# First attention's last output product moved into the second attention's first step, and two sets of flips given to TensorE

## The chip, the cores and the metric

One core of one Trainium2 chip runs the kernel. A core has five engines that work side by side and wait for each other through semaphores: TensorE (PE, matmuls and transposes, with a separate row PEld for its weight loads), VectorE (DVE), ScalarE (ACT), GpSimd (POOL) and SyncE (SP, which here only issues transfers). Transfers are issued by SP or POOL and run on the core's 16 DMA engines. The metric is device microseconds of one execution; the time of a kernel is the median of its runs.

## The reference, cut to what matters

```python
def reference(x, ...):                      # x: 8 batches x 128 tokens x 512
    x = x + attn(cond(x, cond_weight, adapter_ids), wq, wk, wv, wo)
    x = x + ffn(cond2(x, Wq, Wk, Wv, Wo, ..., k_cache, v_cache, block_table, cache_seqlens), ...)
    return x

# cond:  h = x[b] @ weight[adapter_ids[b]].T                   a gathered 512x512 matrix for each batch
# attn:  32 query heads and 8 key heads of 16, causal softmax, output product with wo (512x512)
# cond2: q, k, v from x; RMS norm and rotation of q and k; keys and values are 512 cached rows,
#        gathered by pages, and the 128 own ones; cached rows from cache_seqlens on are masked;
#        softmax over 640; 32 query heads and 8 key heads of 128; output product with Wo (4096 -> 512)
# ffn:   y @ kernel + bias + two low-rank terms, one of them chosen by a gate for each batch
```

All of it is float32.

## The kernel before, in words

The order of the instructions on every engine is the order in which the program text issues them; tiles come from pools with a fixed number of buffers, and a tile waits until the last readers of its buffer are done. Each queue, SP's and POOL's too, works in order.

**Set-up.** SP loads the adapter numbers and the first x, then the first attention's weights wk, wv and wq (`wq_sb`, 1 MB, L368), the norm weights and the FFN bias (L370 to L372). POOL gathers the four 256 KB parts of batch 0's conditioning matrix (L296, tiles `cw`), then those of batch 1, then loads `wo_sb` (1 MB, L355) and two further x.

**First attention**, two half steps for each batch b (`for k in range(2 * B + 1)`): conditioning product (L515, `hp`), query, key and value products (L531, L546, L553), scores with a causal mask (L584, L596), softmax on DVE and ACT (L605, L619, L628), the division on POOL (L630), transposes of the probabilities on PE (L639), the value product (L658) and, one batch later, `out_proj1` (L674 to L679): four products of the attention's result `oT1` with `wo_sb`, the sum with x on DVE, and a store of the sum, `x1`, to DRAM (`x1_kept`). `flip_x1` (L683) makes the transposed copy `x1T` that the second attention reads. The tiles of this half lie in the pools `p1w` and `p1`, which are closed before the second half opens `p2c` and `p2` over the same memory. The last batch's `out_proj1` and `flip_x1` stand just ahead of that, after `keys(0)` and around `own_keys(0)`. On the way the weights of the second attention's first two heads are loaded (`load_qkv`, `load_wo`), and the FFN's low-rank terms are merged (`merge_a`, `merge_b`, `merge_w`).

**Second attention**, one step for each of 64 units u, a unit being one key head of one batch; heads 2n and 2n+1 of a batch make a pair, whose cached keys and values come in one gather (L158, POOL). In step u stand, on PE's order: the scores of unit u (L871 against the cached keys, L878 against the own ones), with the query product of unit u+1 (L175) between them; its key and value product (L215); the value product of unit u-1 (L927); transposes of unit u+1's queries (L252) and own keys (L271); the output product of unit u-1 (L946), summed into `y_acc`. DVE masks and negates the scores (L884), ACT takes the exponentials and divides (L894, L862), and DVE and POOL rotate and scale unit u+1's queries and keys (L198 to L245).

Two kinds of 128x128 flips are made without PE. The probabilities: DVE transposes 32x32 blocks (L865, tile `flips`), and SP moves the blocks to their places with 16 transfers of 80 KB for each unit (L915, tile `pT`). The cached keys of a pair: DVE block transposes (L822, `turn_keys`), then 16 transfers of 32 KB on SP (L835, `move_keys`), in a step of its own for pair 1 (all sixteen in step 1) and eight for each step after. Only units 0 and 1 have their keys flipped by PE (`keys`, L263, copied by ACT, L265).

**The end.** When the last head of a batch is done, `ffn_flip` transposes `y_acc` (L959, L961), `ffn_lora` takes the low-rank product (L978), `ffn` the main one (L993, L994) and adds the residual, which `ffn_loads` has fetched back from DRAM (L967 to L971). For batch 7 these follow each other in three steps without any scores.

## Time and profile before

| | us |
|---|---|
| median of 3 runs | 1432.43 |
| lowest and highest | 1428.14, 1433.11 |
| the profiled execution | 1425.07 |
| its span | 1423.3 |
| PE busy in it | 1390.3 (98%) |
| DVE busy | 935.1 (66%) |
| ACT busy | 653.3 (46%) |
| POOL busy | 566.7 (40%) |
| from one step's value product to the next, typical | 17.8 |

The span runs from the first instruction of the program to the last; 1.8 us of the profiled execution lie around it. The typical step is read from the chain that ended last, where the value products (L927) of steps 6 and 7 start at 340.18 and 357.97. A line of the profile such as `L927 PE MATMUL op<-pT,vg` names the line of the kernel, the engine, the operation, and the tile written and those read, with buffer numbers left out. Idle time in brackets is that of the engine before the instruction, with what ended it; where a wait has several conditions, the profile names the one whose semaphore it saw last. PE's granted clock is a share of full speed.

### The profile page before, as it was taken

What the parts mean: (1) busy time and instruction counts of PE and PEld (TensorE: products, weight loads), DVE (VectorE), ACT (ScalarE), POOL (GpSimd) and SP (SyncE); (2) the same over time, 40 slices, a digit from 0 to 9 for tenths busy, and PEclk for the clock granted to TensorE, in tenths of its full rate; (3) what the DMA queues carried; (4) which work ended last, traced back from release to release, by engine and by line L of the source; (5) the groups of instructions that cost most, each with busy time, mean ns of one, the idle gap of its engine ahead of it and who ended that gap; (6) DMA issues with size and microseconds to landing.
All of it is one profiled execution on the core that took longest, in us unless ns stands there. A gap on an engine that the chain in (4) does not pass through costs nothing.

```text
span 1423.3 us, 20224 instructions
## 1 busy us (share of the span) xinstructions
PE 1390.3 (98%) x6192; PEld 895.2 (63%) x6192; DVE 935.1 (66%) x2270; ACT 653.3 (46%) x1514; POOL 566.7 (40%) x552
## 2 busy tenths in 40 slices
PE   6999998999999999999999999999999999999997
PEld 6877754566666666666666666666666666566654
DVE  4777856566666666666666666666666766566651
ACT  3655534444444444444444444444444444334440
POOL 5774342433333333333333333333333433333220
PEclk9999999999999999999999999999999999999999
DMA  6255112444444565444445654444456544444332
GB/s 205 76 157 195 43 47 65 140 118 119 118 118 118 163 189 153 119 119 118 119 119 159 195 150 119 119 118 118 121 163 192 158 109 125 136 116 115 104 109 66
DMA packets 159387, 181.84 MB, mean 128 GB/s; under 512 B 94960, under 2 KB 100336, under 8 KB 159280
## 3 DMA queue, kind: packets, MB, share of 16 engines
q1 hardware_dynamic: 144000, 137.02, 34.2%
q0 software_dynamic: 15280, 43.53, 10.8%
q8 instruction: 50, 0.82, 0.3%
q14 instruction: 57, 0.47, 0.1%
HBM read 75.57 MB, written 4.72 MB: 56 GB/s over the span
## 4 chain that ended last, share of the span: by engine, by line
PE 91%; SPq 3%; DVE 2%; issue 2%; DMA 1%; POOL 1%; ACT 1%; DVEq 0%; POOLq 0%; ACTq 0%
PE op L927 19%; PE qp L175 15%; PE sc L871 15%; PE yp L946 15%; PE kvp L215 7%; PE sc L878 4%; PE hp L515 2%; SPq L915 2%; PE qTp L252 2%; PE att L674 2%; PE fp L993 2%; PE pT1p L639 2%; PE qp L531 2%; PE o L658 1%; PE sc L596 1%
## 5 line engine op out<-in xcount | busy, mean ns | idle before, releaser
L884 DVE CUSTOM_DVE_ANT_0 pr<-sc,mask,nq 128x640 f32<-128x640 f32 x256 | 225.8, 883 | 141.0 <-PE sc L878 128.1
L894 ACT ACTIVATE pr<-pr,nm 128x640 f32<-128x640 f32 x256 | 211.8, 827 | 188.0 <-DVE nm L884 185.2
L871 PE MATMUL sc<-kT,qT 128*128 128x512 f32 x512 | 263.2, 596 | 1.9 <-ACT kTo L273 1.5
L175 PE MATMUL qp<-wq,x1T 128*128 128x512 f32 x512 | 251.2, 593 | 0.0
L927 PE MATMUL op<-pT,vg 128*128 128x256 f32 x1024 | 244.6, 382 | 5.6 <-DMA pT<-fl 5.6
L946 PE MATMUL yp<-wo,oT 128*128 128x512 f32 x512 | 231.0, 594 | 0.0
L201 POOL TENSOR_TENSOR qa<-qa,qb 128x512 f32<-128x512 f32 x64 | 81.8, 1278 | 370.0 <-DVE sums L861 370.0
L927 PEld LDWEIGHTS op<-pT,vg 128*128 128x128 f32 x1024 | 195.6, 192 | 33.6 <-issue 5.4
L862 ACT ACTIVATE pr<-pr,sums 128x640 f32<-128x640 f32 x256 | 208.4, 814 | 0.0
L865 DVE STREAM_TRANSPOSE fl<-pr 128x640 f32<-128x640 f32 x256 | 192.2, 807 | 1.2 <-DMA kT<-flk 1.0
L878 PEld LDWEIGHTS sc<-kTo,qT 128*128 128x128 f32 x512 | 96.8, 190 | 124.8 <-issue 103.9
L946 PEld LDWEIGHTS yp<-wo,oT 128*128 128x128 f32 x512 | 92.3, 190 | 93.3 <-issue 92.0
L158 POOL DMA_INDIRECT kg<-in_k_cache_dram,idx_kv x128 | 131.6, 1028 | 37.5 <-issue 36.8
L158 POOL DMA_INDIRECT vg<-in_v_cache_dram,idx_kv x128 | 128.4, 1003 | 35.6 <-issue 32.9
L871 PEld LDWEIGHTS sc<-kT,qT 128*128 128x128 f32 x512 | 88.1, 192 | 81.9 <-issue 76.3
L254 ACT COPY qT<-qTp 128x512 f32<-128x512 f32 x64 | 37.5, 586 | 206.7 <-PE qTp L252 206.7
L215 PEld LDWEIGHTS kvp<-wkv,x1T 128*128 128x128 f32 x512 | 97.3, 190 | 40.5 <-issue 30.1
L215 PE MATMUL kvp<-wkv,x1T 128*128 128x256 f32 x512 | 121.0, 379 | 0.0
L242 POOL TENSOR_TENSOR rs<-ss,minus_half 128x5 f32<-128x5 f32 x64 | 76.5, 1195 | 82.4 <-DVE ss L240 82.4
L175 PEld LDWEIGHTS qp<-wq,x1T 128*128 128x128 f32 x512 | 82.8, 191 | 31.5 <-issue 31.5
L878 PE MATMUL sc<-kTo,qT 128*128 128x128 f32 x512 | 99.3, 276 | 0.0
L273 ACT COPY kTo<-kTp 128x128 f32<-128x128 f32 x64 | 17.1, 267 | 167.3 <-PE kTp L271 167.3
(140 smaller groups left out, 1682.0 us busy)
## 6 DMA issues: line engine op xcount, KB each, us to landing
pT<-fl SPq DMA_DIRECT2D x1024, 80.0 KB
kT<-flk SPq DMA_DIRECT2D x496, 32.0 KB
wq<-in_wq_dram SPq DMA_DIRECT2D x8, 1024.0 KB
wo<-in_wo_dram SPq DMA_DIRECT2D x8, 1024.0 KB
wkv<-in_wkv_dram SPq DMA_DIRECT2D x8, 512.0 KB
x_kept<-x SPq DMA_DIRECT2D x8, 256.0 KB
kg<-in_k_cache_dram,idx_kv POOLq DMA_INDIRECT x128, 3.5
vg<-in_v_cache_dram,idx_kv POOLq DMA_INDIRECT x128, 3.6
```

What stands on the lines that cost most here:

```text
L158: nc.gpsimd.indirect_dma_start(out=dst[:, c].rearrange("p n d -> p (n d)"), out_offset=None, in_=src, in_offset=bass.IndirectOffsetOnAxis( ...
L175: nc.tensor.matmul(s["qp"][:].rearrange("p h d -> p (h d)"), x1T[b][:, c, :], weights[g][0][:, c, :], start=(c == 0), stop=(c == KC - 1),)
L201: nc.gpsimd.tensor_tensor(qa[:], qa[:], qb[:], ALU.add)
L215: nc.tensor.matmul(s["kp"][:], x1T[b][:, c, :], weights[g][1][:, c, :], start=(c == 0), stop=(c == KC - 1))
L862: nc.scalar.activation(prs[r][:], prs[r][:], AF.Copy, scale=sums[:, r : r + 1])
L865: nc.vector.transpose(s["flips"][:, :, :, r, :].rearrange("p b c j -> p c b j"), prs[r][:])
L871: nc.tensor.matmul(sc[:, : NBLK * P].rearrange("p (k j) -> p k j", j=32), s["qT"][:, r, :], s["kT"], start=True, stop=True,)
L878: nc.tensor.matmul(sc[:, NBLK * P : NK], s["qT"][:, r, :], s["kTo"][:], start=True, stop=True)
L884: nc.vector.tensor_tensor_reduce(out=pr[:], in0=sc[:, :NK], in1=mask[:], scale=s["nq"][:, r : r + 1], scalar=3.0e38, op0=ALU.add, op1=ALU.min,
L894: nc.scalar.activation(pr[:], pr[:], AF.Exp, bias=nm[:, r : r + 1], scale=-1.0, accum_out=sums[:, r : r + 1],)
L927: nc.tensor.matmul(ops[h][:, : 2 * S], cached(u, "vg", c) if c < NBLK else s["vo"][:], s["pT"][:, :, c, 2 * h : 2 * h + 2, :].rearrange("p ...
L946: nc.tensor.matmul(yp[:], s["oT"][:, r, :], weights[g][2][:, r, :], start=(r == 0), stop=(r == REP - 1))
```

## The change

Four things are edited.

1. *Set-up.* `wq_sb` is loaded by POOL, between the gathers of batch 0 and batch 1, and no longer by SP. The bias is loaded by SP in the first attention's step of batch 4, ahead of `merge_loads`.
2. *The last batch of the first attention.* Its result goes to a tile of its own, `oT_kept`. Its output product is no longer made before the second half, but in step 0, after the products of unit 1 (`out_proj_last`), and its transposed copy later in that step (`flip_last`). x is loaded for it again (`x_last`). `wo_sb` moves to the pool of the second attention's output weights, which has two buffers; so `load_wo(1)`, which stood in the first attention, comes at the end of step 0.
3. *The keys of pair 1* (units 2 and 3) are flipped by PE in step 1, like those of units 0 and 1; DVE's transposes and SP's sixteen transfers for them are gone.
4. *The end.* Unit 63's probabilities are flipped by PE (`flips_last`: five transposes a head, copied to `pT` by DVE and ACT in turn), two heads before the LoRA and output products of unit 62 and two after. `y_acc` of batch 7 is transposed without unit 63's part; unit 63's output product is taken the other way round (`out_proj_turned`, 16 products of 128x128), so that it can be added to the transposed tile. Two steps fewer are run.

```diff
+    oT_kept = one([P, REP, S], F32, "oT_kept")
...
     def keys(u):
         s = st[u]
-        if u > 1:
-            return
...
-        wo_sb = p1w.tile([P, REP, DM], F32, tag="wo_sb", name="wo_sb")
+        wo_sb = wpool.tile([P, REP, DM], F32, tag="wo", name="wo_sb")
...
         gather_w(0)
+        nc.gpsimd.dma_start(out=wq_sb[:], in_=wq1.rearrange("(c p) e -> p c e", p=P))
         gather_w(1)
         nc.gpsimd.dma_start(out=wo_sb[:], in_=wo1.rearrange("(r p) e -> p r e", p=P))
...
-        nc.sync.dma_start(out=wq_sb[:], in_=wq1.rearrange("(c p) e -> p c e", p=P))
...
-        nc.sync.dma_start(out=bias[:], in_=ffn_b.unsqueeze(0).to_broadcast([P, DM]))
...
-                oT[b] = p1.tile([P, REP, S], F32, tag="oT1", name=f"oT1_{b}")
+                oT[b] = p1.tile([P, REP, S], F32, tag="oT1", name=f"oT1_{b}") if b + 1 < B else oT_kept
...
                 elif b == 3:
                     load_qkv(1)
-                    load_wo(1)
...
                 if b == 4:
+                    nc.sync.dma_start(out=bias[:], in_=ffn_b.unsqueeze(0).to_broadcast([P, DM]))
                     merge_loads()
         keys(0)
-        out_proj1(B - 1)
         own_keys(0)
         for i in range(2, KC):
             merge_w(i)
-        flip_x1(B - 1)
...
+    x_last = p2c.tile([P, DM], F32, tag="res", name="x_last")
+    nc.sync.dma_start(out=x_last[:], in_=x[B - 1])
+
+    def out_proj_last():
+        ps = p_mm.tile([P, DM], F32, tag="mm", name="att1_last")
+        for r in range(REP):
+            nc.tensor.matmul(
+                ps[:], oT_kept[:, r, :], wo_sb[:, r, :], start=(r == 0), stop=(r == REP - 1)
+            )
+        x1 = tile_a([P, DM], "x1_last")
+        nc.vector.tensor_tensor(x1[:], ps[:], x_last[:], ALU.add)
+        nc.sync.dma_start(out=x1_kept[B - 1][:], in_=x1[:])
+        return x1
+
+    def flip_last(x1):
+        tp = p_tp.tile([P, KC, S], F32, tag="tp", name="x1Tp_last")
+        for c in range(KC):
+            nc.tensor.transpose(tp[:, c, :], x1[:, c * P : (c + 1) * P], ident[:])
+        nc.scalar.copy(x1T[B - 1][:], tp[:])
...
-        if u in (1, 2):
+        if u == 2:
             turn_keys(u)
-        if 0 < u < N - 2:
-            for a in range(4) if u == 1 else range(u % 2 * 2, u % 2 * 2 + 2):
+        if 1 < u < N - 2:
+            for a in range(u % 2 * 2, u % 2 * 2 + 2):
                 move_keys(u // 2 + 1, a)
...
         divide(REP - 1)
+        s["pT"] = p2.tile([P, 4, NBLK + 1, REP, 32], F32, tag="pT2", name=f"pT_{u}")
+        if u == N - 1:
+            s["prs"] = prs
+            return
         for r in range(REP):
             turn(r)
...
+    def flips_last(u, heads):
+        s = st[u]
+        for r in heads:
+            for n, blocks in enumerate((range(NBLK), range(NBLK, NBLK + 1))):
+                tp = p_tp.tile([P, 4, P], F32, tag="tp", name=f"prT_{u}_{r}_{n}")
+                for c in blocks:
+                    nc.tensor.transpose(
+                        tp[:, c % NBLK, :], s["prs"][r][:, c * P : (c + 1) * P], ident[:]
+                    )
+                (nc.vector.tensor_copy, nc.scalar.copy)[(r + n) % 2](
+                    s["pT"][:, :, blocks[0] : blocks[-1] + 1, r, :].rearrange("p a c j -> p c a j"),
+                    tp[:, : len(blocks), :].rearrange("p c (a j) -> p c a j", j=32),
+                )
...
+    def out_proj_turned(u, before):
+        g, b = units[u]
+        yp = p_mm.tile([P, KC, S], F32, tag="mm", name=f"yp_{u}")
+        for c in range(KC):
+            for r in range(REP):
+                nc.tensor.matmul(
+                    yp[:, c, :],
+                    weights[g][2][:, r, c * P : (c + 1) * P],
+                    st[u]["oT"][:, r, :],
+                    start=(r == 0),
+                    stop=(r == REP - 1),
+                )
+        nc.vector.tensor_tensor(before[:], yp[:], before[:], ALU.add)
...
-    for u in range(N + 3):
+    for u in range(N + 1):
...
         flipped = [(b, ffn_flip(b)) for b in pending]
+        if u == N:
+            flipped.append((B - 1, ffn_flip(B - 1)))
         if last:
             values(u - 1)
+        if u == N - 1:
+            flips_last(u, (0, 1))
+        if u == 0:
+            x1_last = out_proj_last()
         if nxt:
             norms(u + 1)
             queries(u + 1)
-            keys(u + 1)
+            for v in {0: (1,), 1: (2, 3)}.get(u, ()):
+                keys(v)
...
+        if u == N:
+            out_proj_turned(u - 1, flipped[-1][1])
         flipped = [(b, yT, ffn_lora(b, yT)) for b, yT in flipped]
-        if last:
+        if last and u < N:
             for r in range(REP):
                 out_proj(u - 1, r)
+        if u == N - 1:
+            flips_last(u, (2, 3))
+        if u == 0:
+            flip_last(x1_last)
         if nxt:
             own_keys(u + 1)
+        if u == 0:
+            load_wo(1)
```

More of the change, by code (lines that the diff above doesn't have):

```diff
@@ L908, in scores @@
         divide(REP - 1)
+        s["pT"] = p2.tile([P, 4, NBLK + 1, REP, 32], F32, tag="pT2", name=f"pT_{u}")
+        if u == N - 1:
+            s["prs"] = prs
+            return
         for r in range(REP):
             turn(r)
-        s["pT"] = p2.tile([P, 4, NBLK + 1, REP, 32], F32, tag="pT2", name=f"pT_{u}")
         for a in range(4):
@@ L1056, in block_kernel @@
             ffn_loads(0)
-        pending = [units[u - 1][1]] if last and units[u - 1][0] == NKV - 1 else []
+        pending = [units[u - 1][1]] if last and u < N and units[u - 1][0] == NKV - 1 else []
 def kernel(
```

## The prediction

> **What bounds the kernel now.** I read the page first, then the list of waits of TensorE (PE), then the instructions in order of time where those waits lie, then the clock and the DMA share in short windows. The page's first part:
>
> ```profile
> span 1423.3 us, 20224 instructions
> ...
> PE 1390.3 (98%) x6192; PEld 895.2 (63%) x6192; DVE 935.1 (66%) x2270; ACT 653.3 (46%) x1514; POOL 566.7 (40%) x552
> ```
>
> PE is the bound: 33.0 us (1423.3 - 1390.3) are all it ever idles, so only those, time at a reduced clock, and PE work itself can be saved. The waits of PE (us in total, times, longest) name the large ones:
>
> ```profile
> PE op L927 <- DMA pT<-fl: 5.6, 3, 3.4
> PE hp L515 <- DMA cw<-in_cond_w_dram,idx_w: 5.6, 2, 4.2
> ...
> PE kTp L271 <- DVE ka L245: 2.7, 1, 2.7
> ...
> PE sc L871 <- ACT kTo L273: 1.5, 1, 1.5
> ```
>
> None recurs in the 64 steps of the second attention; they lie at the start, around steps 0 to 2, and in the last two steps. The instructions there (start, duration, in brackets the idle time before and what ended it):
>
> ```profile
> 6.54 0.38 SPq L368 DMA_DIRECT2D wq_sb<-in_wq_dram  x1
> 14.47 0.84 POOL L355 DMA_DIRECT2D wo_sb<-in_wo_dram  x1
> 14.83 3.54 PE L515 MATMUL hp<-xT,cw 128*128 128x128 f32 x16 [1.39 <-DMA cw<-in_cond_w_dram,idx_w]
> 20.93 3.74 PE L531 MATMUL qp<-hT,wq_sb 128*128 128x128 f32 x32
> 214.83 3.60 PE L674 MATMUL att<-wo_sb,oT 128*128 128x512 f32 x8
> 220.38 0.66 PE L500 MATMUL x1Tp<-ident,x 128*128 128x128 f32 x4
> 221.65 0.56 POOL L810 IOTA place_i<- 128x512 int32 x1 [19.25 <-ACT x1T L683]
> 236.95 0.45 PE L271 MATMUL kTp<-ident,ka 128*128 128x128 f32 x1 [2.73 <-DVE ka L245]
> 257.94 1.10 PE L871 MATMUL sc<-kT,qT 128*128 128x512 f32 x2 [1.49 <-ACT kTo L273]
> 1401.44 3.75 PE L927 MATMUL op<-pT,vg 128*128 128x256 f32 x8 [3.38 <-DMA pT<-fl]
> ```
>
> Windows (stretch, its length, busy us of PE, PEld, DVE, ACT, POOL; then granted clock, DMA share, GB/s):
>
> ```profile
> 16.00:18.00 2.00, 2.00 (x12) 2.00 (x11) 0.00 (x0) 0.00 (x0) 1.44 (x2) 1.00 1.02 156
> ...
> 237.00:239.00 2.00, 2.00 (x4) 0.97 (x5) 0.27 (x1) 0.27 (x1) 1.57 (x2) 0.50 0.59 169
> ...
> 1402.00:1404.00 2.00, 2.00 (x6) 1.64 (x5) 0.00 (x0) 0.00 (x0) 0.84 (x1) 0.50 0.58 194
> ```
>
> So two of the waits cost twice: after them the clock stands at 0.50 for some 3.4 us.
>
> **Part 1, the start.** Today the 1 MB of wq_sb leaves SP at 6.54, among the first four gathers of POOL (issued 4.15 to 8.16). The second half of the first conditioning product waits 1.39 for the third gather. In the new order wq_sb follows the fourth gather on POOL, at about 9.6. The gathers took 5.3 us at the least from issue to landing; the third, issued at 6.88, then lands at about 12.2, before PE ends the first half at 13.4. **-1.4**, no more, as PE is busy from 9.68. Low end 0: the norm-weight loads (issued 7.39 and 8.19) no longer stand behind wq_sb and may fall on the gathers; the window at 16 us has full DMA engines at 156 GB/s, which I put down to such broadcast loads. I take -1.4, because the third gather may be 1.2 us late at no cost. wq_sb itself is first read at 20.93 - 1.4 = 19.5; the x loads of POOL's queue, issued just behind the like-sized wo_sb, took 9.2 us to land, and 9.6 + 9.2 = 18.8. POOL's issues behind it slip by 1.1 (0.84 and the gap of 0.3): the last gather of the second weights, issued 13.53, took some 7.5, so 22.1 instead of 21.0; it is read at 26.6 - 1.4. Hidden. The bias leaves the start; its first reader is POOL's L968, some 900 us behind its new place.
>
> **Part 2, the seam.** Before step 0 the four products of L674 and the four transposes of L500 leave PE: 3.43 (start to start) + 0.48 = 3.9. The pools of the second half reuse memory that these held, so POOL's place_i (and the mask, and the first softmax pass at 223.49) waited until 221.65; now the last value products (done 214.4) free it, and the 0.37 that step 0's third scores waited for that pass goes too. **-4.3.** The new x_last load sits on SP ahead of the pT moves, is free to go at about 214.5, and has 12 us to land.
>
> At step 0's end PE ends kvp at 231.16 and then idles 1.07, 0.68 and 2.73 around three short transposes, for VectorE's (DVE's) chain to ka. The moved product fills that hole. Clock from kvp's end: att 0 to 3.4, queries 3.9, cached keys 4.4, the flip of x1 waits for the copy of qT (0.6) and runs to 5.2. DVE gets one more add (0.69) ahead of the norms: 3.7 to 4.4, then ss 0.2, POOL's power 1.2, nq and ka 0.5: ka at 6.3, kTp at 6.35 against 5.79 today. **+0.5.** But PE now idles 1.4 there instead of 4.5, so the clock should hold: from the first to the third scores, step 1 took 4.34 (237.19 to 241.53), step 2 3.10 (257.94 to 261.04). **-1.3.**
>
> [...] The trace has 1.35 us of idling at 1383.9 with the clock still 1.00, and 0.50 after 3.38 us without any work; a stretch of transposes and short waits as here it does not have. [...]
>
> Step 1: pair 1's keys. DVE loses four stream transposes (1.41) and SP sixteen issues (245.13 to 255.5). The 1.49 that step 2's scores waited is named ACT's, but kTo was done at 257.14; the last kT transfer, issued at 254.9, is what ended. It goes. Against it: eight transposes (1.0) and a wait for the copy of qT (0.35), +1.35, and kTo behind the y copy of ScalarE (ACT), up to 0.2. ACT's two more copies (0.59 each) lie in its idle 2.85 before the y copy (253.54 to 256.39). **0.** The pT moves of step 1 no longer queue behind sixteen kT issues, so step 2's value products lose their 0.84 (kept apart: their rule is the 16 pT issues of 0.63, landing 2.1 later). **-0.8.** SP's store of x1 and the 1 MB of wo_1 (0.7 to issue) now stand between the pT moves of steps 0 and 1: the first are out at about 240, the second are ready at 245.8, wo_1 is read in step 2, over 20 us on. Step 0's pT landed 2.0 before use; 0.8 of that is eaten, 1.2 left. Seam: -4.3 + 0.5 - 1.3 + 0 - 0.8 = **-5.9**; range -4 (clock drops, longer waits) to -6.8.
>
> **Part 3, the end.** Today after unit 62's value products (1389.6): output product 3.5, FFN 4.45 (1393.61 to 1398.06), wait 3.38, value products at half clock 7.4, output product 3.6, then add, transpose, copy and LoRA product one behind the other 2.5 (1412.28 to 1414.75), FFN 4.55 to 1419.3: 29.7. New: twenty transposes at 0.12 (L639: eight in 1.04) are 2.4; two PSUM buffers serve eight copies on DVE and ACT in turn, so about four times PE waits for a copy (0.3 each beyond what runs meanwhile): 1.1. Flips 1.5, LoRA and output product 3.9, flips 1.7 (with the y add ahead of a copy on DVE), FFN 4.3, the flip of y 0.45, value products at full clock 4.3, output product turned round 3.65 (32 matmuls like L531) and 0.25 for the second half's copy, add 0.8, LoRA product 0.4, FFN 4.5: 25.8. **-3.9.** The copies that regroup columns are not in the trace; nearest is L935 (128x256 in 0.42), so I take 0.7 for 128x512; at twice that PE waits 1.4 more. DVE's four transposes of step 63 (3.0) and SP's 16 issues go. The loads of res and b_rep leave after unit 6's result at about 1402 as today, land by 1407 and are read at 1414. Range -2 to -5.
>
> **Sum.** -1.4 - 5.9 - 3.9 = -11.2 against the profiled execution: 1425.07 (span 1423.3 and 1.8 around it) becomes 1413.9. The median of the runs shown is 7.4 higher, 1432.43, with the same work; I carry the difference over: **1421.2 us**. Steps 3 to 61 have the same instructions on every engine and are costed at nothing.
>
> **The rivals.** (a) *Half of it*: [...]the flips' copies cost double (+1.4) and the gathers stay late (+1.4). For: two of three have no row here. Against: each has cover named above. 1425.5. (b) *The transfers do not matter*: if the pT waits at the end only hide another wait (b_rep, or DVE's add), the end gains 0.5 instead of 3.9: 1424.6. Against: the loads' times above. (c) *Slower*: in every step the pT moves arrive late. Place: L927, steps 3 to 61. In step 3 they are out at 281.8 and landed 2.1 later, the value products start at 286.37: 2.5 in hand. If the SP queue's changed rotation ate that and 0.2 more a step, 59 x 0.2 = 11.8 would swallow the gain: 1433; at 0.4 a step 1445. For: every engine follows this wait when it comes. Against: SP's list per step is unchanged. It decides from 2.7 us of delay. (d) *The change does not do what it says* at the start: the load on POOL's queue lands late, PE waits at L531 instead: beyond 19.5 each us costs one; 1422.6 to 1424 if the gain is lost.
>
> **How the numbers follow.** Forecast 0.62, (a) 0.12, (b) 0.09, (c) 0.05, (d) 0.12. Own range of the forecast 1417 to 1426: parts at their far ends give -6.5 to -13.5, and runs of one kernel spread over 5 us (1428.14 to 1433.11). With the cases 1415 to 1429. Half a per cent is 7.2 us, about what a measurement of this kernel can tell: faster means below 1425.3. Forecast 0.57 of its 0.62, (d) 0.10, (a) and (b) 0.10 together: 0.77; slower (c), 0.04; the rest 0.19 within.
>
> **What the profile after would show.** Right: no wait of hp for the third gather and the L531 product about 1.4 earlier; kvp of step 0 followed at once by att_last, the clock 1.00 at the start of step 1; no wait of sc in step 2 or of op in steps 2 and 64; clock 1.00 in the last 25 us; steps 3 to 61 at 17.8. Wrong: qp waiting for wq_sb, a clock of 0.50 in step 1, waits of over 0.5 between the prT transposes, or any wait of op that recurs.

## The result, and the profile after

The changed kernel takes 1420.66 us (median of six runs, 1420.12 to 1423.96); the kernel before, run beside it, 1430.37 us (six runs, 1427.59 to 1433.11). The ratio is 0.9937 with a 95% interval of 0.992 to 0.9954: faster by 0.63%, 9.0 us. The medians as they stand lie 9.7 us apart; where a difference of medians and a ratio disagree, the text goes by the ratio, which has an interval. The forecast was 1421.2 us, 11.2 us off 1432.43. Part of so close a hit is luck: the later runs of the kernel before came out 2 us lower, and the gain itself is about 2 us smaller than forecast. A second comparison, on another chip (run a_after below), gave 0.9941 (0.9929 to 0.9953), 8.4 us of 1423.66. One execution of e4's second comparison below took 1829 us at a mean clock of 0.75 and is left out.

The kernel after was profiled twice. The first profile's page, and the waits of PE in it (total us, times, longest):

```profile
span 1421.1 us, 20290 instructions
...
PE 1391.5 (98%) x6244; PEld 898.5 (63%) x6244; DVE 931.8 (66%) x2266; ACT 655.9 (46%) x1520; POOL 568.2 (40%) x553
```

```profile
PE pT1p L638 <- DVE pT L644: 3.6, 1, 3.6
PE yp L982 <- DVE oT L971: 2.0, 1, 2.0
...
PE op L963 <- DMA pT<-fl: 1.6, 1, 1.6
PE kTp L271 <- DVE ka L247: 1.1, 1, 1.1
```

Of the forecast's targets, the waits of op fell from 5.6 us to 1.6 and that of kTp from 2.7 to 1.1; the wait of step 2's scores (1.5) is gone. But two waits are new, the first two lines, and the change edits neither instruction: one at 184 us in the last half step of the first attention, one at 272 us in step 2. The second profile, of the same program on another chip, has neither:

```profile
span 1414.1 us, 20290 instructions
```

```profile
PE hp L514 <- DMA cw<-in_cond_w_dram,idx_w: 5.3, 2, 4.1
...
PE qTp L254 <- POOL qa L203: 2.4, 1, 2.4
PE op L963 <- DMA pT<-fl: 1.6, 1, 1.6
...
PE kTp L271 <- DVE ka L247: 1.1, 1, 1.1
```

So I read the steps from this second profile and come back to the two new waits below (after the kernels before and after again, and in e3). Its seam, PE in order of time (start, duration, in brackets the idle time before and what ended it):

```profile
226.51 3.60 PE L820 MATMUL att_last<-wo_sb,oT_kept 128*128 128x512 f32 x8
229.94 0.60 PE L254 MATMUL qTp<-ident,qa 128*128 128x128 f32 x4
230.38 0.60 PE L263 MATMUL kgTp<-ident,kg 128*128 128x128 f32 x4
231.22 0.66 PE L831 MATMUL x1Tp_last<-ident,x_last 128*128 128x128 f32 x4 [0.24 <-ACT qT L256]
232.93 0.30 PE L271 MATMUL kTp<-ident,ka 128*128 128x128 f32 x1 [1.06 <-DVE ka L247]
233.07 1.02 PE L889 MATMUL sc<-kT,qT 128*128 128x512 f32 x2
...
236.10 1.02 PE L889 MATMUL sc<-kT,qT 128*128 128x512 f32 x2
...
252.19 1.02 PE L889 MATMUL sc<-kT,qT 128*128 128x512 f32 x2
...
261.82 1.89 PE L963 MATMUL op<-pT,vg 128*128 128x256 f32 x8
```

The moved product fills the hole in which PE idled 4.5 us; 1.3 us of idling are left. From the first to the third scores of step 1 it is 3.03 us (236.10 - 233.07) where it was 4.34, and windows over the hole and behind it (length, busy us of PE, PEld, DVE, ACT, POOL, then granted clock, DMA share, GB/s) have the clock at full:

```profile
231.00:233.00 2.00, 0.72 (x5) 0.52 (x6) 0.64 (x4) 1.24 (x3) 1.65 (x2) 1.00 0.45 109
233.00:235.00 2.00, 2.00 (x7) 1.06 (x8) 0.90 (x2) 0.27 (x1) 1.55 (x2) 1.00 0.66 181
```

Step 2's scores (252.19) and value products (261.82) follow the work ahead of them with no idle time. The end, in the same view:

```profile
1379.47 1.96 PE L963 MATMUL op<-pT,vg 128*128 128x256 f32 x8 [1.57 <-DMA pT<-fl]
...
1384.93 0.77 PE L948 MATMUL prT<-ident,pr 128*128 128x128 f32 x5 [0.36 <-ACT pT L951]
...
1390.58 0.81 PE L948 MATMUL prT<-ident,pr 128*128 128x128 f32 x5 [0.36 <-ACT pT L951]
...
1395.96 1.89 PE L963 MATMUL op<-pT,vg 128*128 128x256 f32 x8
...
1400.28 4.07 PE L997 MATMUL yp<-oT,wo 128*128 128x128 f32 x32
1405.20 0.43 PE L1029 MATMUL axp<-yT,a_eff 128*32 128x128 f32 x8 [0.85 <-DVE yT L1004]
...
1409.09 1.02 PE L1045 MATMUL fp<-b_rep,ax 128*128 128x512 f32 x2
```

The flips cost PE two waits of 0.36; the last value products start as soon as the flip of y is through, at 1.89 us for eight where they took 3.75 at half clock.

How much earlier than in the first profile of before does the same work of PE start? (After: the second profile.)

| work of PE | before, us | after, us | earlier by | step alone |
|---|---|---|---|---|
| first product with wq_sb | 20.93 | 20.89 | 0.0 | start 0.0 |
| last value product of the first attention | 214.03 | 214.01 | 0.0 | |
| first scores of step 0 | 220.87 | 216.92 | 4.0 | |
| last scores of step 0 | 226.48 | 221.98 | 4.5 | 4.5 |
| kTp ahead of step 1 | 236.95 | 232.93 | 4.0 | -0.5 |
| value products in step 1 | 248.00 | 242.56 | 5.4 | 1.4 |
| first scores of step 2 | 257.94 | 252.19 | 5.8 | 0.3 |
| value products in step 2 | 268.51 | 261.82 | 6.7 | 0.9 |
| kTp ahead of step 48 | 1078.20 | 1071.44 | 6.8 | 0.1 |
| kTp ahead of step 52 | 1152.21 | 1146.23 | 6.0 | -0.8 |
| unit 62's value products | 1385.23 | 1379.47 | 5.8 | -0.2 |
| last product of the FFN | 1418.71 | 1409.52 | 9.2 | 3.4 |

Start (0), seam (6.74) and end (3.44) make 10.2 us. From step 3 to step 48 nothing moves by more than 0.1 us. The 0.8 lost between steps 48 and 52 is a wait which both kernels have and whose length changes from one execution to the next (1.65 us in one profile of before, 2.12 in the other, 2.44 here); e8 takes it up.

One pair of profiles is one pair of executions, and the runs below let the same stretches be read in more of them:

| stretch of PE | old form, us | new form, us |
|---|---|---|
| up to the first scores of the first attention | 25.3 to 26.2, mean 25.7 (seven profiles) | 23.9 to 25.7, mean 24.9 (five) |
| last value product of the first attention to value products of step 3 | 73.0 (before, twice), 73.4 to 74.3 (e1 and both of e4) | 66.3 (second of after, e5 to e8), 70.2 (first of after) |
| unit 62's value products to the last product of the FFN | 33.4 to 33.6 (before, twice, and e2), 32.1 (e1, e3, e5) | 30.05 or 30.06 (both of after and of e4, e6 to e8) |

So the start is worth some 0.8 us on average where the pair shows none, the seam 6.7 to 8.0, and the end 3.4 or 2.0. The two sizes of the end go with the clock: in the traces of the 33.4 to 33.6 it stands at 0.50 for 6.83 us around the last value products, in those of the 32.1 for 3.41. Both profiles of before have the longer.

### The profile page after: what moved, and what is told of

Read it like the earlier page. It is cut to its first block, busy times and chain, and to the rows that moved or that the text cites. A ratio compares the mean times of both kernels' runs of the same rounds, so it can differ in the third digit from the quotient of the medians.

```text
span 1421.1 us, 20290 instructions
## 1 busy us (share of the span) xinstructions
PE 1391.5 (98%) x6244; PEld 898.5 (63%) x6244; DVE 931.8 (66%) x2266; ACT 655.9 (46%) x1520; POOL 568.2 (40%) x553
## 4 chain that ended last, share of the span: by engine, by line
PE 93%; DVE 2%; issue 2%; DMA 1%; ACT 1%; POOL 1%; SPq 1%; another core or an unknown queue 0%; DVEq 0%; POOLq 0%; ACTq 0%
PE op L963 19%; PE qp L177 15%; PE sc L889 15%; PE yp L982 15%; PE kvp L217 7%; PE sc L896 4%; PE fp L1044 2%; PE hp L514 2%; PE qTp L254 2%; PE pT1p L638 2%; PE qp L530 2%; PE att L673 2%; PE o L657 1%; PE sc L595 1%; PE kvp L545 1%
## 5 line engine op out<-in xcount | busy, mean ns | idle before, releaser
L883 DVE STREAM_TRANSPOSE fl<-pr 128x640 f32<-128x640 f32 x252 | 189.2, 808 | 0.0
L160 POOL DMA_INDIRECT vg<-in_v_cache_dram,idx_kv x128 | 128.6, 1005 | 37.8 <-issue 33.6
```

The lines of the kernel that those rows point to most:

```text
L160: nc.gpsimd.indirect_dma_start(out=dst[:, c].rearrange("p n d -> p (n d)"), out_offset=None, in_=src, in_offset=bass.IndirectOffsetOnAxis( ...
L883: nc.vector.transpose(s["flips"][:, :, :, r, :].rearrange("p b c j -> p c b j"), prs[r][:])
```

## The experiments

Ratios are to the kernel before, run beside each on the same chip, with 95% intervals. The first four ran on one chip, the next four on a second, the last four on a third. The medians of before there were 1428.93, 1423.66 and 1423.57 us, so times of different groups are not to be compared. The intervals are up to 0.27% of the time wide, 3.9 us from end to end: a part that is worth 1 us can be seen, if at all, in several profiles, not in these times.

### e1: the start alone

```diff
         gather_w(0)
+        nc.gpsimd.dma_start(out=wq_sb[:], in_=wq1.rearrange("(c p) e -> p c e", p=P))
         gather_w(1)
...
-        nc.sync.dma_start(out=wq_sb[:], in_=wq1.rearrange("(c p) e -> p c e", p=P))
```

with the bias load moved as in the change.

> Only the start of the change on the kernel before: the query weights on POOL's queue between the first gathers, the bias load later. By the steps of the prediction: the wait of hp for the third gather (1.39 us) goes, the qp product starts 1.4 us earlier or, as in the profile of after, 2.4 us earlier, of which the wait of the first scores for VectorE's qT gives 1.2 back: -1.2 to -1.4 us at the end of the first attention, 1429.1 against a before of 1430.4. Rival, the gain is absorbed on the way (the first attention's last half step waits again, as at 184 us in the profile of after, where PE waited 3.6 us): 0 or slower by up to 3.5 us. If that wait of 3.6 us belongs to the new order of the start, it shows here; if it is a chance of one execution, it does not.

Measured: 1.0002 (0.9991 to 1.0013). The third gather's wait was still there, 1.30 us where it was 1.39. PE in order of time:

```profile
9.69 3.76 PE L514 MATMUL hp<-xT,cw 128*128 128x128 f32 x16 [4.14 <-DMA cw<-in_cond_w_dram,idx_w]
14.75 2.05 PE L514 MATMUL hp<-xT,cw 128*128 128x128 f32 x16 [1.30 <-DMA cw<-in_cond_w_dram,idx_w]
19.36 3.74 PE L530 MATMUL qp<-hT,wq_sb 128*128 128x128 f32 x32
```

The qp product does start 1.57 us earlier than in before's profile, but not by the mechanism I named: the second half of the product ran at full clock (2.05 us for sixteen) instead of half (3.54). In the second profile of after it ran at half again (3.78 us) and nothing was gained. The trace's first record of the clock, 1.00, stands at 13.9 us here, at 18.0 in before, at 18.5 in the second profile of after and at 12.8 in e6. Ahead of it none is recorded (windows print 1.00 there), and "half" is read from the pace: before's first sixteen products, at 9.68 us, took 3.75. What moves the rise, no run here tests. Of the 1.57 us, 1.05 were lost again at the first scores, which waited 1.6 us for VectorE's qT. The wait at 184 us is here too; e2, e3 and e4 keep the old start and have it as well, so it does not come from the new one.

### e2: the moved output product alone

oT_kept, the weights' pool, out_proj_last and flip_last as in the change; pair 1's keys still by VectorE and SP.

```diff
-        out_proj1(B - 1)
         own_keys(0)
...
-        flip_x1(B - 1)
...
+        if u == 0:
+            x1_last = out_proj_last()
...
+        if u == 0:
+            flip_last(x1_last)
```

> Only the moved output product (with its kept oT, the weights' pool and the flip of x1) on the kernel before. By the steps: -4.3 (product and transposes leave PE ahead of step 0) +0.5 (kTp later) -1.3 (the clock stays at 1.00 in step 1) = -5.1 us: 1425.3 against 1430.4, scores of step 1 at 3.1 us from first to third. [...] Rival, a stall of some 4 us at about 263 us (step 2) comes with the move: -1 us.

Measured: 0.9963 (0.9949 to 0.9976), -5.3 us. Step 0 starts 3.9 us earlier against the work ahead of it, kTp is 1.06 us late as in the whole change, and the clock holds in step 1 (scores at 1.02 us from the start): the three terms of -4.3, +0.5 and -1.3 stand. (e2's profile has the late hand-over at 184 us, so step 1 begins at the same moment as in before: kTp at 236.93 and 236.95.) The profile has one thing that the expectation had not, a wait ahead of step 2's scores of 2.92 us where before had 1.49:

```profile
258.31 2.02 PE L891 MATMUL sc<-kT,qT 128*128 128x512 f32 x2 [2.92 <-issue]
```

The last of SP's sixteen key moves was issued at 255.09 us, in before at 254.87. SP issues without a break from 233.35 us on: the sixteen pT moves, then the edit's own store of x1 and load of wo_1, which hold it 1.1 us, then the keys. What PE gains ahead of this list, it waits for there, and pays again at the clock, which was 0.59 in the window from 258 to 260 us. This execution was the slowest of e2's seven (1426.40 us, the others 1423.58 to 1425.38), so the others may have waited less.

### e3: pair 1's keys by TensorE alone

```diff
-        if u > 1:
-            return
...
-            keys(u + 1)
+            for v in {0: (1,), 1: (2, 3)}.get(u, ()):
+                keys(v)
...
-        if u in (1, 2):
+        if u == 2:
             turn_keys(u)
```

> Only pair 1's keys by TensorE on the kernel before. By the steps: eight transposes and the wait for their copy +1.35, the wait of step 2's scores -1.49, the wait of step 2's value products for pT -0.84: -0.8 to -1.1 us, 1429.5 against 1430.4; no wait of over 0.5 us of sc or op in step 2. Rival: the moved product makes room for these transposes, and alone they only lengthen PE's work: +0.3 to +1.3 us. If the stall at about 263 us in the profile of after belongs to the keys, it shows here.

Measured: 1.0018 (1.001 to 1.0026), slower by 2.6 us; its profile is 1.3 us slower from the last half step to step 3. The terms are as expected: the output product of step 1 1.33 us later, then -1.65 at the scores of step 2 and -0.9 at its value products. What the profile lost lies beside them:

```profile
242.65 0.45 PE L269 MATMUL kTp<-ident,ka 128*128 128x128 f32 x1 [2.73 <-DVE ka L245]
242.89 1.91 PE L869 MATMUL sc<-kT,qT 128*128 128x512 f32 x2
245.03 1.92 PE L869 MATMUL sc<-kT,qT 128*128 128x512 f32 x2
...
248.69 1.02 PE L869 MATMUL sc<-kT,qT 128*128 128x512 f32 x2
...
264.78 1.02 PE L869 MATMUL sc<-kT,qT 128*128 128x512 f32 x2
```

The hole ahead of kTp is still open, and the half clock behind it lasted longer than in before (5.80 us from the first to the third scores against 4.34: +1.46); and in step 2 the output product waited 0.89 us for VectorE, which cost 1.1. The first of these is not the edit's doing: e1 and both profiles of e4, which leave these steps as they were, have 5.43, 4.83 and 4.94 us there, and their traces the same 6.83 us at a clock of 0.50 (before: 3.41). Against e1 and the first of e4, on the same chip, e3's profile is only 0.0 and 0.5 us slower from the last half step to step 3. The second is the wait that after's first profile has at 272 us (2.00 us there). Those two profiles, both with pair 1's keys on PE and both with late signals at 184 us, are the only ones with it; e1, e2 and e4 have none, nor has any profile of the other two chips. Whether it makes up the 2.6 us is not shown: 22 timed runs say that the edit alone costs time on this chip, and the profile does not say where. The recorded rival (+0.3 to +1.3 us) comes nearer than the steps: alone, the edit does not pay.

### e4: the end alone, in two comparisons

flips_last, out_proj_turned and the loop's end as in the change.

> Only the end of the change on the kernel before: the last probabilities flipped by TensorE and the last output product turned round. By the steps -3.9 us, by the profile of after -3.4 to -3.7: 1426.8 against 1430.4; from the end of unit 62's value products to the end of the last FFN product 26.2 us against 29.7, clock 1.00 throughout. Rival, the transfers do not matter: -0.5 us, another wait of 2 to 3 us takes the place of the one for pT.

> Only the end of the change on the kernel before, a second time: in the first its profile showed the gain of 3.4 to 3.7 us in the last two steps, its timed runs no gain (0.9998). If the end is worth what its profile shows, the ratio is 0.9976 here, and the first comparison was spoilt by waits elsewhere that came and went (the late hand-over at 184 us and others). If the timed runs were right, 1.000, and the profile of the end will show where the gain is given back.

Measured: 0.9998 (0.9989 to 1.0006) and 0.9997 (0.9989 to 1.0005), with 14 and 13 runs: no gain that can be told from noise. Both profiles show one. From the start of unit 62's value products to the last FFN product, before takes 33.48 us (1418.71 - 1385.23), e4 30.05 in both of its profiles: -3.4. Ahead of that they lose 0.5 between kTp of unit 63 and these value products, where the profile shows a longer wait for the moved probabilities (1.82 for 1.35), and 0.5 in steps 2 to 52. But before's profiles both have the longer half clock at the end. Against the three profiles with the shorter one (32.1 us: e1, e3, e5) the end gains 2.0, and with the two losses taken off, 1.0 to 2.4 us are left for the whole. The low end of that lies within both intervals, which reach to -1.6 us; what the timed runs had, no trace tells. Before's two profiles (1425.07 and 1426.05 us) also lie 1.4 and 2.4 us above the median of the runs beside them (1423.66), e4's second (1423.86) close to its own (1423.41). So the gain of the end in its own stretch is shown in every profile that has it; that the end alone shortens the whole is not shown. The whole change (0.9941) and e5, which keeps the old end and the old start (0.9964), have intervals that just touch at 0.9953.

### The kernels before and after again

> The kernel before, unchanged, for a second profile. Its first profile (1425.07 us) is below nearly all of its timed runs; the four kernels with one part each all show a wait of PE of 3.6 us for VectorE's pT at about 184 us, and lie 3.3 to 5.7 us late from there, that first profile does not. If this late hand-over is a habit of all these programs, it is here too: span 1427 to 1428, step 0 begins about 4 us later than in the first profile. If it comes with any change of the program, it is not here: span 1423.

> The kernel after, unchanged, for a second profile. The first showed the wait of 3.6 us at 184 us and a second late hand-over in step 2 at 263 us (loss 4.0 us), and was the slowest of six runs (1423.96 against 1420.1 to 1422.4). If the second is a chance of one execution and the first a habit, this profile shows the wait at 184 us and none at 263 to 272 us, with a span of about 1418; if both are habits, 1421.

Measured: before 1.0003 (0.9991 to 1.0014), as it must be, span 1424.3; after 0.9941, span 1414.1. Neither shows the 3.6 us at 184 us or the 2.0 us in step 2. So the alternatives that I had written down, a habit of all these programs or a matter of changed ones, are both wrong: the first four experiments ran on one chip, and there every profile has the late hand-over at 184 us; on the two other chips none of eight profiles has it (the chip of after's first profile is not on record). How it looks, first in e4 on the first chip, then in before on the second (VectorE and PE in order of time):

```profile
185.11 0.42 DVE L465 COPY a_eff<-aeff 128x256 f32<-128x256 f32 x1 [3.87 <-PE pT1p L639]
...
187.75 1.16 PE L639 MATMUL pT1p<-ident,pr 128*128 128x128 f32 x8 [3.58 <-DVE pT L645]
```

```profile
182.07 0.42 DVE L465 COPY a_eff<-aeff 128x256 f32<-128x256 f32 x1 [1.30 <-PE aeff L458]
...
185.07 1.16 PE L639 MATMUL pT1p<-ident,pr 128*128 128x128 f32 x8 [0.44 <-DVE pT L645]
```

PE's products are at the same pace in both, 0.216 us each, but in the first the semaphore signals by which VectorE learns of them come 1.2 to 3.8 us after the products' recorded ends (in the first profile of after the third group ended at 182.26 and its signal stands at 185.55). The same traces lack a fifth of the recorded signals: 875 of 1113 of PE's are there in the first profile of after, all of them in the second. What makes the signals late, and whether it is also what loses the records, no run tests. What matters for the verdict is that the delay comes with no part of the change (e1 to e4 all have it), and that the ratio is much the same with it in after's profile (0.9937) and without (0.9941).

### e5: the seam whole

e2 and e3 together.

> The moved output product and pair 1's keys by TensorE together on the kernel before. By the steps of the prediction and the profile of after -5.9 to -6.7 us: 1422.2 to 1423 against 1428.9. If the parts only add up as they were measured alone (-4.1 for the product, +3.1 for the keys against 1428.9), 1428: then the gain of the whole does not lie at the seam. If the keys cost time alone only because PE stood at half clock in step 1, the pair gives what the product gives alone or more: 1424.9 or less.

Measured: 0.9964 (0.9953 to 0.9975), -5.1 us. Its profile gains 6.7 us from the last half step to step 3, to the tenth what the whole change gains there; e2 alone gained 3.0 in its profile, and e3 alone lost 1.3. In the profiles, then, the pieces need each other: without the keys on PE the gain of the moved product waits for SP's key moves in step 2, and without the product in the hole the half clock in step 1 stays. The timed runs do not bear that out: e2 alone gave as much as the pair by the ratios (0.9963 and 0.9964), and 1.2 us less by the medians (-4.1 and -5.3 us), which is within the noise. The sum of the parts as timed, -2.7 us, lies outside e5's interval (-3.6 to -6.7), but the parts have intervals of their own and were run on another chip, so that the parts do not add up is likely and not shown.

### e6: the value gathers later

```diff
                     gather(0, "kg")
-                    gather(0, "vg")
...
     nc.gpsimd.memset(place[:, NBLK * P :], -3.0e38)
+    gather(0, "vg")
```

> The kernel after, with one edit: the four gathers of pair 0's values, which POOL issues behind the four of its keys from 179 to 184 us, are issued behind the mask's preparation at about 219 us. Nothing reads them before step 1 (about 246 us). If the run of eight gathers is what makes PE's signals to VectorE late at 180 to 186 us, the wait of 3.6 us shrinks to under 1 and the half clock behind it goes: -3 to -4.8 us against after, 1416 to 1418. If the gathers have nothing to do with it: 1420.7, wait unchanged.

Measured: 0.9944 (0.9931 to 0.9957), the same as after. It says nothing on its question, since on its chip the late hand-over does not occur with the gathers in their old place either. It did show that the four gathers may stand 40 us later at no cost that can be seen.

### e7: the norm weights out of the start

```diff
         wn = [both.tile([P, D2], F32, tag="kb", name=f"wn_{n}") for n in range(2)]
-        nc.sync.dma_start(out=wn[0][:], in_=qn_w.unsqueeze(0).to_broadcast([P, D2]))
-        nc.sync.dma_start(out=wn[1][:], in_=kn_w.unsqueeze(0).to_broadcast([P, D2]))
...
                 if b == 0:
+                    nc.sync.dma_start(out=wn[0][:], in_=qn_w.unsqueeze(0).to_broadcast([P, D2]))
+                    nc.sync.dma_start(out=wn[1][:], in_=kn_w.unsqueeze(0).to_broadcast([P, D2]))
                     indices()
```

> The kernel after, with one edit: the two loads of the norm weights (64 KB each, in packets of 512 bytes read again and again) leave the start and are issued in the first attention's second half step; their first reader comes in the fourth. In the second profile of after the third gather landed at 14.5 us as before the change, although the query weights no longer stood ahead of it, and those small packets held the DMA engines from 10 to 12.5 us. If they are the cause, the wait of 1.2 to 1.4 us inside the first hp product goes, the product takes 6.4 us in one go and all that follows is 1.6 to 2.4 us earlier: ratio to before 0.9941 - 0.0014 = 0.9927. If the gathers are bound by their own bytes (the DMA engines are full from 9 to 21 us either way), the wait only gets smaller by under 0.5 us and the ratio stays at 0.994.

The start in the second profile of after, PE in order of time and then windows:

```profile
14.54 3.78 PE L514 MATMUL hp<-xT,cw 128*128 128x128 f32 x16 [1.21 <-DMA cw<-in_cond_w_dram,idx_w]
```

```profile
10.00:11.00 1.00, 1.00 (x7) 1.00 (x7) 0.97 (x2) 0.00 (x0) 0.70 (x2) 1.00 1.13 108
11.00:12.00 1.00, 1.00 (x6) 1.00 (x6) 0.93 (x3) 0.00 (x0) 0.70 (x2) 1.00 1.00 81
```

and in e7:

```profile
9.79 6.64 PE L512 MATMUL hp<-xT,cw 128*128 128x128 f32 x32 [4.28 <-DMA cw<-in_cond_w_dram,idx_w]
```

```profile
10.00:11.00 1.00, 1.00 (x6) 1.00 (x7) 0.97 (x2) 0.00 (x0) 0.70 (x2) 1.00 0.97 352
11.00:12.00 1.00, 1.00 (x6) 1.00 (x6) 0.93 (x3) 0.00 (x0) 0.70 (x2) 1.00 0.90 217
```

With full DMA engines after moved 108 and 81 GB/s, e7 352 and 217. The third gather landed at 11.70 us instead of 14.50, and the wait inside the product is gone, here and in e8; of the five profiles with the new start and the norm weights in their old place four have it (1.21 to 1.41 us, all but the first of after). The packets in the traces agree. The norm weights' 256 packets of 512 bytes, one row each read 128 times, moved from 13.05 to 17.96 us in before, behind wq_sb, and from 8.48 to 13.49 in the second profile of after, among the gathers. There they took 0.157 us each, 40.2 us of the engines' time or 2.5 us of all sixteen; the 1024 packets of the same size of wk and wv, ahead of the gathers, took 0.027 us each. So the cause of the wait is settled: the norm weights stood on the gathers.

What that is worth is less sure. The first scores start 1.9 us earlier than in the second profile of after (23.61 and 25.50), but in e6, with the wait still there, they start 1.6 earlier:

```profile
14.65 2.05 PE L514 MATMUL hp<-xT,cw 128*128 128x128 f32 x16 [1.37 <-DMA cw<-in_cond_w_dram,idx_w]
...
23.88 1.15 PE L595 MATMUL sc<-kbd,qT 32*128 32x256 f32 x16 [0.54 <-DVE qT L540]
```

In e6 the second half of the product found the clock at 1.00 (recorded from 12.8 us on). The mean of e7 and e8 is 23.4 us, that of the five profiles of the new start 24.9: about 1.5. Measured: 0.9933 (0.992 to 0.9945). Its ratio is the lowest here, but its interval overlaps that of after (0.9941), so that it beats after is not shown in time; that it beats before is.

### e8: and the bias add later

```diff
+    def ffn_bias(b):
+        t = res[b][0]
+        nc.gpsimd.tensor_tensor(t[:], t[:], bias[:], ALU.add)
...
         if u == first:
             ffn_loads(0)
+        if u == first + 1:
+            ffn_bias(0)
```

> The edit of the late norm weights, and one more on the kernel after: POOL's add of the bias to the first residual (L1019), which holds POOL's queue for its load at step 48, is issued one step later. In the profile of after it began at 1103.2 us when the load had landed, POOL's qa behind it at 1104.4, and PE waited 2.4 us for that qa. Theory: this wait goes and with it what half clock follows it in some executions, -1.7 to -2.6 us against the late norm weights alone: ratio to before 0.991. Rival: something else is as late there (the key moves of SP behind the loads), 0 to -0.5 us.

Measured: 0.9938 (0.9925 to 0.9951), no gain over e7. The wait for qa is gone, and two others stand in its place, PE in order of time:

```profile
1106.73 1.10 PE L889 MATMUL sc<-kT,qT 128*128 128x512 f32 x2 [1.27 <-ACT kTo L273]
...
1111.07 1.12 PE L889 MATMUL sc<-kT,qT 128*128 128x512 f32 x2 [1.07 <-DVE nm L902]
```

kTo's copy (0.27 us, behind the flip of 1105.19 to 1105.46) did not end the first; SP issued the last of its key moves at 1103.85, behind the loads of wo, res and b_rep, and it landed at about 1106.6. That is the rival: from step 48 to step 52 e8 loses 1.0 us, the second profile of after 0.8 and e7 2.0, of which 1.7 is a half clock of 3.41 us; that is within what executions differ by.

### e9: do transposes keep the clock up?

```diff
+        if u in (10, 20):
+            tp = p_tp.tile([P, 4, P], F32, tag="tp", name=f"extra_{u}")
+            for c in range(80):
+                if u == 10:
+                    nc.tensor.transpose(tp[:, c % 4, :], ident[:], ident[:])
+                else:
+                    nc.tensor.matmul(tp[:, c % 4, :], ident[:], ident[:], start=True, stop=True)
```

> The kernel after, with 80 more products on PE that nothing reads ahead of the own keys of two steps: 80 transposes by PE in step 10, 80 ordinary products of the same shape in step 20 (8.7 us each at full clock). By the row of the profile (clock 1.00 in step 1 after a stretch with two sets of four and one of four transposes): both stretches run at 1.00, 17.4 us in all, span 1431.5 where after has 1414.1. [...]

One run, 1441.95 us, span 1440.1. The stretch of transposes, and a window from inside it and one over its end:

```profile
413.13 8.90 PE L1109 MATMUL extra<-ident 128*128 128x128 f32 x80
421.86 0.27 PE L271 MATMUL kTp<-ident,ka 128*128 128x128 f32 x1
421.97 1.02 PE L889 MATMUL sc<-kT,qT 128*128 128x512 f32 x2
```

```profile
419.00:421.00 2.00, 2.00 (x21) 2.00 (x20) 0.00 (x0) 0.00 (x0) 0.00 (x0) 1.00 0.34 81
421.00:423.00 2.00, 2.00 (x15) 1.52 (x14) 0.00 (x0) 0.27 (x1) 0.00 (x0) 1.00 0.22 50
```

8.7 us of nothing but transposes, and the granted clock stays at 1.00 to the end and behind it: in this form (128x128, f32) they did not bring it down. It is one execution, and without the short waits of the seam. The span is 9 us above the expectation only because the 80 ordinary products were built as 160 instructions (17.8 us).

## Why the prediction was right, and where not

**Sum.** -11.2 was forecast; the two profiles give -10.2 in the three parts, the two timed comparisons -9.0 and -8.4. Right in the whole, with one step failed. That the parts' misses cancel in part is luck: the seam gave more than forecast, the start and the end less.

**Part 1, the start, failed in its step.** "The third gather then lands at about 12.2" was wrong: it landed at 14.50 us in the second profile of after (14.78 in before), at 14.6 to 14.7 in e1, e6 and e9, and only in the first profile of after at 12.62. The 1 MB of wq_sb was not what kept it late; with it gone, the norm weights came forward onto the gathers. I had written just that as the low end ("may fall on the gathers"), and took -1.4 all the same. e7 shows it by taking those loads away. "No more, as PE is busy from 9.68" was wrong as well: PE was busy there but not at its peak (sixteen products of hp took 3.75 us in before at 9.68, 2.05 in e1 at 14.75), and the first product with wq_sb came 2.4 us earlier in the first profile of after, of which 1.2 reached the first scores. The 0.8 us by which the first scores come earlier on the average of the profiles go, the first of after apart, with the moment at which the clock rises (12.8 to 18.5 us), which the forecast did not have; they do not make its step right. The loads' landing for L531 and POOL's slipped issues were no trouble: wq_sb had landed at 17.87 against a first use at 20.89, and rival (d) is out.

**Part 2, the seam, was right term by term**: -4.5 for the work that leaves PE (forecast -4.3), +0.5 for kTp, -1.4 for the clock (-1.3), -0.3 for the keys (0), -0.9 for step 2's probabilities (-0.8), and 0.1 more after it; -6.7 in all, at the far end of the range that I gave. The price read from the scores (4.34 against 3.10 us) was right about the clock: it stands at 1.00 in every window from 229 to 237 us of the second profile of after, and through e9's transposes. That it might drop there, in the low end of my range, was an estimate, and no profile with the moved product shows it. Two things I had not seen. The clock's term depends on the execution: with the longer half clock, the first to third scores of step 1 take 4.8 to 5.4 us in kernels with the old seam (e1, e4) where before had 4.34. And the 0 for the keys is, once the product has moved, a difference of 3.7 us between the profiles with and without them (e5 and e2), though not between their times.

**Part 3, the end, was right in the profiles, and a little large**: -3.4 for -3.9 against before's profiles, -2.0 against those in which the half clock at the end was the shorter. "The clock stands at 0.50 for some 3.4 us" misread the row: in before's trace it is 6.83 us there, and 3.41 only in step 1. From the first flip to the end of the last FFN product it is 26.2 us (1383.87 to 1410.11) where the forecast had 25.8; the waits for the flips' copies came to 0.7 where I gave 1.1. The forecast's sum has 1.5 and 1.7 for the flips, 0.3 less than the 2.4 and 1.1 that it made them from, and the profile has 1.75 and 1.71; the turned product and the add behind it took 4.9 for 4.7. The copies that regroup columns did not cost double: in the first profile of after a 128x512 takes 0.69 us on DVE and 0.59 on ACT, where I took 0.7. The wait ahead of unit 62's value products grew from 1.35 to 1.57, which I had not counted. Rival (b) is out by the profiles; the timed runs of the end alone (e4) would not rule it out.

**The median.** Carrying over the 7.4 us between before's profile and its runs was right in effect, and blind in its reason: a good part of it seems to be the chip. In the profiles with the late hand-over the stretch from the first scores to the last value products of the first attention is 3.4 to 5.8 us longer than the 187.8 of both profiles of before; on the two chips without it before's median is 1423.6, below its profiles. That the first comparison ran on a chip with it is inferred from after's first profile. The parts' far ends add up to -6.0 and -13.2, where the forecast's range has -6.5 and -13.5; the measured -9.0 lies within either.

**Rivals (a) and (c).** Of (a)'s three items, a clock that drops at step 0's end (an estimate, +1.5), copies at double cost and late gathers, only the last came. Of (c) there is nothing: steps 3 to 48 take the same time in both kernels, to a tenth of a us over 45 steps.

## What to carry to other kernels

When a transfer is taken out from ahead of another, look at what moves up into its place, and count packets beside bytes: here 128 KB in packets of 512 bytes kept the third gather as late (14.50 us) as the 1 MB load ahead of them had (14.78); without them it landed at 11.70 (e7). A gain ahead of a queue that runs to its own time can be lost at the next wait for that queue, as in e2's profile, so see what that queue does next before a move is priced. A wait whose half clock comes and goes has several prices (the one at 184 us cost 3.4 to 5.8 us): read its stretch in more than one profile before its removal is worth a number. And before reading a new wait in a profile as the change's doing, profile the unchanged kernel again on the same chip.

## What the runs showed of the hardware

- 80 transposes by PE in a row (8.7 us) held the granted clock at 1.00 (e9).
- Apart from each trace's own start and end, a half clock lasted 3.41 or 6.83 us wherever a trace has one: 3.41 from 236.4 us and 6.83 from 1400.4 in the first profile of before, 3.41 from 188.2 and from 273.5 in the first of after.
- The length of a wait did not tell whether the clock would drop. The idle stretch of 3.6 us at 184 us dropped it to 0.50 in three of the profiles that have it (e1, e3 and the first of after) and left it at 1.00 in two (e2 and e4). Shorter waits dropped it too: 1.94 us (e7) and 2.60 (e6) at step 48, 2.00 (the first of after) and 2.92 (e2) in step 2; others of 2.12 (the second of before) and 2.44 (the second of after) at step 48 did not. The 3.6 us cost 3.4 without the drop, 4.6 and 4.9 with 3.41 us of it, and 5.8 with 6.83.
- 256 packets of 512 bytes, which read the same two rows again and again among the gathers, took 0.07 us each in the first profile of before, 0.11 in the first of after and 0.16 in the second; 1024 packets of that size ahead of the gathers took 0.03. Whether the repeated rows or the company make the difference, no run here tests.
- On one chip of three, signals from PE to VectorE came up to 3.8 us late at one place of every profile, together with traces that lack a fifth of the signals (875 of 1113 of PE's are there in the first profile of after).
